# One value product for two heads on 64x64 tiles, with copies on ScalarE and TensorE steps of 640 instructions

## The chip, the cores and the metric

The kernel runs on one core of a Trainium2 chip. The metric is the device time in microseconds (us) of one execution. Before the change three runs took 4342.97, 4343.37 and 4332.03 us; the median is 4342.97 us. A further execution was profiled, and all views below are of it.

## The reference

A layer of two parts works on x, two images of 128 channels and 256x256 pixels, all in fp32.

```
x = x + conv_ref(ln_c(x), W_qkv, W_out, rel_height, rel_width)    # attention in windows
t = tokens of x
t = t + ffn_ref(ln_t(t), router_w, router_b, expert_w, expert_b)  # 8 experts, the best 2 weighted
```

In `conv_ref` the queries of an 8x8 window look at the keys and values of the 12x12 window around it, in 4 heads of 32 channels. A fixed mask leaves to each query only the keys whose row and column offsets have one parity. With it the window falls apart into four planes (row parity, column parity), in each of which 16 queries (4x4) look at 36 keys (6x6). The softmax of the scores weights the values, and `W_out` maps the result back:

```
attn = softmax(q @ k + rel_pos_emb + FIXED_MASK)
out  = attn @ v              # per window and head
return W_out @ out
```

In `ffn_ref` a router gives 8 probabilities per token, and the two best experts' outputs are added with normalised weights.

## The kernel before

The image is cut into strips of 8 rows, 64 strips over both images. Each strip has four parity planes, so the main loop makes 256 steps n. A plane of a strip has 4 rows and 128 columns: 512 queries, 32 windows of 16. Windows are taken in pairs whose key ranges are merged (6 rows, 10 columns, 60 keys in a slot of 64 partitions): 16 pairs, 8 in each half of the strip.

The order of work is written out by hand. The body of the loop advances generators (`next(score)`, `next(ahead)`, `next(attn)`, `next(norm)`, `next(outp)`) and interleaves them with the experts of an earlier row pair and with loads and stores; on every engine and in SP's DMA queue instructions run in that order. For TensorE a step n is:

- `scores` (L476, L493): the position terms of plane n, then the products of keys and queries. A tile takes 32 rows and 64 columns of the array; 4 heads and 2 halves make 8 tiles.
- `project` for plane n+1: values (`value_rows`, L349), relative logits (L408), keys (L422) and queries (L447), with the whole array.
- four expert products (L716) into the accumulator `acc`.
- `attend`: the softmax denominators (L514, the lhs is a block of ones with 32 columns), then the value products (L524, called PV below), one for each pair of windows, half and head: 64 products, each on 64 rows (keys) by 32 columns (the head's channels), with 32 queries streamed.
- the norm sums of a row (L582), three expert products (L716), the output projection `po` of plane n (L552), and the eighth expert product.

An fp32 product is two weight loads and two matmuls in the profile (PEld and PE), so the 64 value products are 128 of each.

PSUM tile `att` (4 banks, one buffer) holds the scores in its columns 0 to 255. ScalarE turns them to `pT` by one exp (L501). The value products and the denominators are then written to the columns 256 to 511 of the same tile (`av`). VectorE transposes the denominators (`sT`, L534), takes reciprocals (`rc`, L536), transposes them back (`rT`, L539) and multiplies: `o` = values times `rT` (L544). `o` is the moving operand of `po`. In the loop these three parts of `attend` stand at three places:

```
next(attn, None)      # L514 and the first half of L524
...                   # expert inputs xe on VectorE, DMA issues
next(attn, None)      # the second half of L524, sT, rc
next(attn, None)      # rT, o
```

ScalarE's order around this place is: the squares for the norm sums (L576), then what follows `next(attn)`, the one-column copy that paces the load of x (L114, its DMA is L115 on SP), later Ln and Exp for the norm (L235, L236).

From step 6 on each step begins with a directive to the loader (L825): it fills TensorE's instruction stream with empty slots until the next instruction lies at `BLOCK - FIRST_LIMIT` modulo `BLOCK`. With `BLOCK, FIRST_LIMIT = 256, 99` (L47) the first 99 instructions of a step are the last of a group of 256.

Of the kernel before, what the change touches and what calls it, by code (L numbers as in the profile page):

```python
# [13 lines left out]
ALU = mybir.AluOpType  # L14
# [4 lines left out]
HEADS, DH = 4, 32  # L19
# [24 lines left out]
KR, KC = 6, 10  # L44
NK = KR * KC
SLOT = 64
BLOCK, FIRST_LIMIT = 256, 99  # L47
NU = 9


# [1 line left out]
def kernel(  # L52
# [16 lines left out]
    nc = tc.nc  # L69
# [6 lines left out]
    HQ = NQ // 2  # L76
# [18 lines left out]
    def ctile(shape, name):  # L95
        return const.tile(shape, F32, tag=name, name=name)
# [48 lines left out]
    ones = ctile([P, 32], "ones")  # L145
# [28 lines left out]
    for rname, rsb in zip(("relh", "relw"), relsb):  # L174
# [4 lines left out]
        rT = ctile([P, n_rel], f"{rname}T")  # L179
# [6 lines left out]
    for h in range(HEADS):  # L186
        hp = slice(h * DH, (h + 1) * DH)
# [317 lines left out]
    def attend(n, state):  # L505


        att, pT, vv = state["att"], state["pT"], state["vv"]
        av = att[:, :, HQ:512]
        for half in range(2):  # L510
            rows = slice(half * SLOT, (half + 1) * SLOT)
            for h in range(HEADS):
                hp = slice(h * DH, (h + 1) * DH)
                nc.tensor.matmul(  # L514
                    av[hp, 2 + half], lhsT=ones[rows, :], rhs=pT[rows, h], start=True, stop=True
                )
        for t in range(HP):
            if t == HP // 2:
                yield
            for half in range(2):  # L520
                rows = slice(half * SLOT, (half + 1) * SLOT)
                for h in range(HEADS):
                    hp = slice(h * DH, (h + 1) * DH)
                    nc.tensor.matmul(  # L524
                        av[hp, half, 32 * t : 32 * t + 32],
                        lhsT=vv[rows, t, hp],
                        rhs=pT[rows, h, 32 * t : 32 * t + 32],
                        start=True,
                        stop=True,
                    )  # L530


        sT = work.tile([P, 2, HQ], F32, tag="sT", name=f"sT{n}", bufs=1)
        nc.vector.transpose(sT, av[:, 2:4])  # L534
        rc = small.tile([P, NQ // 32], F32, tag="rc", name=f"rc{n}")
        nc.vector.reciprocal(rc, sT.rearrange("p f (b k) -> p (f b) k", k=32)[:, :, 0])  # L536
        yield
        rT = work.tile([P, 2, HQ], F32, tag="rT", name=f"rT{n}", bufs=1)
        nc.vector.transpose(  # L539
            rT.rearrange("p f (b k) -> p (f b) k", k=32),  # L540
            rc.unsqueeze(2).broadcast_to([P, NQ // 32, 32]),
        )
        o = work.tile([P, 2, HQ], F32, tag="o", name=f"o{n}")
        nc.vector.tensor_tensor(o, av[:, 0:2], rT, ALU.mult)  # L544
        state["o"] = o
        yield

# [262 lines left out]
    with tc.manual_schedule(engines={ET.PE, ET.DVE, ET.Activation, ET.Pool, ET.SP}):  # L810
        for n in range(n_planes + 7):
            i, pl = divmod(n, 4)
            score, attn, outp, ahead, norm, rout = none, none, none, none, none, none
            if n < n_planes:
                score = scores(n, states[n])
                attn = attend(n, states[n])
                outp = out_project(n, states[n])
# [21 lines left out]
            if gated:  # L839
                f, c, made = gated  # L840
# [15 lines left out]
            f = (i - 1, pl) if 0 < i <= len(strips) else None  # L856
# [107 lines left out]
```

## Time and profile before

| | |
|---|---|
| median of 3 runs | 4342.97 us (4332.03 to 4343.37) |
| profiled execution, its own time | 4328.49 us |
| its span, first to last instruction | 4326.7 us |
| TensorE matmul busy | 4223.3 us, 98% |
| VectorE busy | 3791.0 us, 88% |
| ScalarE busy | 1320.7 us, 31% |
| L524, value products, matmuls | 32768, 346.7 us busy, mean 200 ns |
| L514, denominators, matmuls | 4096, 169.6 us busy, mean 388 ns |
| L544, o | 256, 177.0 us busy, mean 691 ns |
| mean granted TensorE clock | 0.991 |

Matmuls overlap one another, so a mean duration is longer than the distance from one start to the next; starts are what counts in a row of them. A timeline line gives start, length, engine, line, operation, tiles, form and count, and in brackets the idle time before it with what ended it. "issue" there is time in which the engine waited for nothing that the profile shows. Queue q8 carries instruction blocks to the engines; its packets are in the trace with start and length.

### The profile page before, as it was taken

To read this page: it belongs to the slowest core of one execution; us is meant where nothing else is said; L and a number is where in the kernel's file an instruction comes from. 1 tells how busy PE (TensorE), PEld (TensorE's weight loads), DVE (VectorE), ACT (ScalarE), POOL (GpSimd) and SP (SyncE) were. 2 spreads that over 40 slices of the span, in tenths; PEclk is the share of its full clock that TensorE was granted. 3 is DMA by queue.
4 is the path that set the end of the run, shared out by engine and by line. 5 is a ranking of instruction groups with operands and counts; after the bars stand their busy time and mean duration, and the time that the engine had idled before them with its cause. 6 is when DMAs were issued, how large, how long until landed. Compare 5 with 4: busy or idle time off the path is not lost. (4 is left out here: it accounts for less than half of the span.)

```text
span 4326.7 us, 224393 instructions
## 1 busy us (share of the span) xinstructions
PE 4223.3 (98%) x94273; PEld 2472.0 (57%) x94273; DVE 3791.0 (88%) x11850; ACT 1320.7 (31%) x3774; POOL 1087.6 (25%) x1126
## 2 busy tenths in 40 slices
PE   7899999999999999999999999999999999999987
PEld 5455555555555555555555555555555555555553
DVE  5788988988888889988888998898998889899877
ACT  3233332332323232333333233233332333333321
POOL 1222222222222222222222222222222222222211
PEclk8999999999999999999999999999999999999999
DMA  3777778787788778777778778778788787787866
GB/s 109 214 234 247 241 244 244 244 247 235 244 236 242 240 243 248 239 246 239 247 237 247 248 240 247 239 244 250 239 248 244 239 249 237 248 243 244 243 191 193
DMA packets 824578, 1022.17 MB, mean 236 GB/s; under 512 B 137634, under 2 KB 409634, under 8 KB 823594
## 3 DMA queue, kind: packets, MB, share of 16 engines
q1 hardware_dynamic: 822864, 1007.52, 75.9%
q8 instruction: 769, 12.60, 1.2%
q14 instruction: 215, 1.76, 0.1%
q10 hardware_dynamic: 730, 0.29, 0.0%
HBM read 863.78 MB, written 143.75 MB: 233 GB/s over the span
## 5 line engine op out<-in xcount | busy, mean ns | idle before, releaser
L716 PE MATMUL acc<-xe,ew 128*128 128x512 f32 x4096 | 1917.9, 601 | 18.6 <-DVE gb L690 14.3
L716 PEld LDWEIGHTS acc<-xe,ew 128*128 128x128 f32 x4096 | 758.4, 190 | 939.7 <-issue 873.1
L707 DVE TENSOR_TENSOR xe<-xs,gb 128x512 f32<-128x512 f32 x1536 | 950.8, 687 | 11.6 <-DMA gb<-gd 1.5
L711 POOL COPY last<-xe 128x1 f32<-128x1 f32 x256 | 47.6, 186 | 3115.3 <-DVE gb L690 3082.2
L707 POOL TENSOR_TENSOR xe<-xs,gb 128x512 f32<-128x512 f32 x512 | 652.3, 1275 | 1.5 <-PE att L524 1.2
L493 PE MATMUL att<-qs,kcol 32*64 32x32 f32 x32768 | 402.1, 227 | 15.8 <-issue 15.4
L493 PEld LDWEIGHTS att<-qs,kcol 32*64 32x64 f32 x32768 | 397.5, 132 | 19.6 <-issue 18.9
L275 POOL TENSOR_TENSOR xn<-xt,rb 128x512 f32<-128x512 f32 x249 | 374.3, 1503 | 94.6 <-DMA rb<-gd 94.0
L524 PEld LDWEIGHTS att<-pT,vwin 64*32 64x32 f32 x32768 | 349.4, 105 | 42.0 <-issue 4.5
L501 ACT ACTIVATE pT<-att 128x1024 f32<-128x1024 f32 x256 | 262.2, 1024 | 298.8 <-PE att L493 298.8
L524 PE MATMUL att<-pT,vwin 64*32 64x32 f32 x32768 | 346.7, 200 | 2.7 <-issue 1.5
L349 PE MATMUL pv<-wt,xn 128*128 128x128 f32 x2048 | 303.8, 292 | 0.6 <-issue 0.6
L412 DVE STREAM_TRANSPOSE uT<-pu 128x512 f32<-128x512 f32 x256 | 183.6, 717 | 134.9 <-PE pu L408 134.9
L576 ACT ACTIVATE sq<-xt 128x512 f32<-128x512 f32 x505 | 292.6, 630 | 0.0
L396 DVE STREAM_TRANSPOSE au<-auT 128x512 f32<-128x512 f32 x256 | 269.6, 1053 | 9.0
L552 PE MATMUL po<-o,wt 128*128 128x512 f32 x512 | 263.6, 596 | 10.2 <-DVE o L544 6.6
L433 ACT COPY kcol<-pk 128x560 f32<-128x560 f32 (+2 forms) x344 | 183.5, 533 | 275.0 <-PE pk L422 272.2
L408 PE MATMUL pu<-xn,wrel 128*128 128x512 f32 x512 | 267.2, 604 | 0.0
L447 PE MATMUL pq<-xn,wt 128*128 128x512 f32 x512 | 262.1, 592 | 1.7 <-issue 1.7
L422 PE MATMUL pk<-xn,wt 128*128 128x512 f32 (+2 forms) x528 | 261.5, 579 | 0.0
L349 PEld LDWEIGHTS pv<-wt,xn 128*128 128x128 f32 x2048 | 254.1, 195 | 11.5 <-issue 1.0
L476 PEld LDWEIGHTS att<-au,keys 32*64 32x64 f32 x8192 | 117.6, 132 | 228.2 <-PE po L552 183.8
(2437 smaller groups left out, 4856.6 us busy)
## 6 DMA issues: line engine op xcount, KB each, us to landing
gb<-gd SPq DMA_DIRECT2D x2048, 256.0 KB, 5.6
vwin<-vrows SPq DMA_DIRECT2D x512, 240.0 KB, 5.1
xt<-in_x_dram SPq DMA_DIRECT2D x256, 256.0 KB, 6.6
sb<-gd SPq DMA_DIRECT2D x256, 256.0 KB, 4.4
out_dram<-xt SPq DMA_DIRECT2D x256, 256.0 KB, 6.0
rb<-gd SPq DMA_DIRECT2D x249, 256.0 KB, 3.4
vrows<-vr SPq DMA_DIRECT2D x168, 256.0 KB, 3.8
vrows<-vr SPq DMA_DIRECT2D x160, 128.0 KB, 3.6
```

What stands on the lines that cost most here:

```text
L275: eng.tensor_tensor(xn[i % 2][:, :, :, k, 1 : PC + 1], ln1_src(i, k).rearrange("p (y j x) -> p y x j", y=2, x=2), rb.rearrange("p (y j x) ...
L349: nc.tensor.matmul(pv[:, j * P : (j + 1) * P], lhsT=xp[:, k, 1 : PC + 1], rhs=wv, start=True, stop=True,)
L396: nc.vector.transpose(au.rearrange("p m a s -> p a s m"), auT[n % 2])
L408: nc.tensor.matmul(pu, lhsT=wrel, rhs=inner, start=True, stop=True)
L447: nc.tensor.matmul(pq, lhsT=wq, rhs=inner, start=True, stop=True)
L493: nc.tensor.matmul(sc[rows, h, 32 * t : 32 * t + 32], lhsT=kk[hp, half * HP + t, :], rhs=qs[hp, m0 : m0 + 2].rearrange("p m a s -> p (m a ...
L501: nc.scalar.activation(pT, att[:, :, 0:HQ], AF.Exp)
L524: nc.tensor.matmul(av[hp, half, 32 * t : 32 * t + 32], lhsT=vv[rows, t, hp], rhs=pT[rows, h, 32 * t : 32 * t + 32], start=True, stop=True,)
L552: nc.tensor.matmul(po, lhsT=wo, rhs=state["o"].rearrange("p f z -> p (f z)"), start=True, stop=True)
L576: nc.scalar.activation(sq, src, AF.Square)
L707: eng.tensor_tensor(self.xe[e], self.xs, self.gb.pop(e), ALU.mult)
L716: nc.tensor.matmul(self.acc, lhsT=ew[:, e, :], rhs=self.xe.pop(e), start=(e == 0), stop=not self.xe)
```

## The change

The value products of two heads become one. The weights are the 64 channels of heads 2g and 2g+1, the moving operand is the 32 queries of both heads side by side (64 columns), and the output is 64 partitions by 64 columns: 32 products, on four tiles of 64 rows by 64 columns. Of each output half the elements are of use: for the even head's partitions the first run of 32 columns, for the odd head's the second. The outputs fill banks 0 and 1 of `att` from column 0, where the scores were. Two ScalarE copies (heads 1 and 3), from PSUM to PSUM, put the odd heads' runs over the mixed ones, so that `o` can read the first runs of all partitions. The denominators keep their place. `BLOCK` becomes 128 and `FIRST_LIMIT` 88.

```diff
-BLOCK, FIRST_LIMIT = 256, 99
+BLOCK, FIRST_LIMIT = 128, 88
...
-        av = att[:, :, HQ:512]
+        av = att[:, 2:4, HQ:512]
+        own = att[:, 0:2].rearrange("p f (t j z) -> p f t j z", j=2, z=32)
...
-                    av[hp, 2 + half], lhsT=ones[rows, :], rhs=pT[rows, h], start=True, stop=True
+                    av[hp, half], lhsT=ones[rows, :], rhs=pT[rows, h], start=True, stop=True
...
-                for h in range(HEADS):
-                    hp = slice(h * DH, (h + 1) * DH)
+                for g in range(2):
+                    gp = slice(2 * g * DH, 2 * (g + 1) * DH)
                     nc.tensor.matmul(
-                        av[hp, half, 32 * t : 32 * t + 32],
-                        lhsT=vv[rows, t, hp],
-                        rhs=pT[rows, h, 32 * t : 32 * t + 32],
+                        att[gp, half, 64 * t : 64 * t + 64],
+                        lhsT=vv[rows, t, gp],
+                        rhs=pT[rows, 2 * g : 2 * g + 2, 32 * t : 32 * t + 32],
...
-        nc.vector.transpose(sT, av[:, 2:4])
+        nc.vector.transpose(sT, av)
...
+        for h in (1, 3):
+            hp = slice(h * DH, (h + 1) * DH)
+            nc.scalar.copy(own[hp, :, :, 0], own[hp, :, :, 1])
...
-        nc.vector.tensor_tensor(o, av[:, 0:2], rT, ALU.mult)
+        nc.vector.tensor_tensor(
+            o.rearrange("p f (t z) -> p f t z", z=32),
+            own[:, :, :, 0],
+            rT.rearrange("p f (t z) -> p f t z", z=32),
+            ALU.mult,
+        )
```

## The prediction

> **What bounds the kernel now.** I read the page's engine shares first, then TensorE's timeline over one step, then the places where that timeline breaks, and last the packet records of the instruction queue.
>
> ```profile
> span 4326.7 us, 224393 instructions
> PE 4223.3 (98%) x94273; PEld 2472.0 (57%) x94273; DVE 3791.0 (88%) x11850; ACT 1320.7 (31%) x3774; POOL 1087.6 (25%) x1126
> ...
> q8 instruction: 769, 12.60, 1.2%
> ```
>
> TensorE is busy 98% of the span. The next view is its timeline over one step (start, length, line, count of matmuls).
>
> ```profile
> 1728.28 0.69 PE L476 MATMUL att<-au,keys 32*64 32x128 f32 x32
> 1728.77 1.53 PE L493 MATMUL att<-qs,kcol 32*64 32x32 f32 x128
> 1730.22 1.16 PE L349 MATMUL pv<-wt,xn 128*128 128x128 f32 x8
> 1731.22 1.02 PE L408 MATMUL pu<-xn,wrel 128*128 128x512 f32 x2
> 1732.08 1.02 PE L422 MATMUL pk<-xn,wt 128*128 128x512 f32 x2
> 1732.94 1.02 PE L447 MATMUL pq<-xn,wt 128*128 128x512 f32 x2
> 1733.80 3.59 PE L716 MATMUL acc<-xe,ew 128*128 128x512 f32 x8
> 1737.33 0.66 PE L514 MATMUL att<-pT,ones 64*32 64x256 f32 x16
> 1737.78 1.34 PE L524 MATMUL att<-pT,vwin 64*32 64x32 f32 x128
> 1739.05 0.43 PE L582 MATMUL plt<-xt,rw 128*32 128x128 f32 x8
> ...
> 1744.55 0.69 PE L476 MATMUL att<-au,keys 32*64 32x128 f32 x32
> ```
>
> There is no gap in it. The step takes 16.27 us, and 153 of the 248 steps with this sequence take that to 15 ns. TensorE is a hard floor, and what is added to or taken from its stream moves every step. The mean step is 16.50 us; the rest is stalls. Two kinds matter here, one in the step at 1065.73, one in the step at 1082.96:
>
> ```profile
> 1066.22 0.37 PE L493 MATMUL att<-qs,kcol 32*64 32x32 f32 x17
> 1067.36 1.34 PE L493 MATMUL att<-qs,kcol 32*64 32x32 f32 x111 [0.78 <-issue]
> ...
> 1088.48 1.45 PE L716 MATMUL acc<-xe,ew 128*128 128x512 f32 x3
> 1090.64 2.31 PE L716 MATMUL acc<-xe,ew 128*128 128x512 f32 x5 [0.71 <-issue]
> ```
>
> "issue" means that no semaphore held it. Count instructions (each product is two weight loads and two matmuls): L476 64, L493 256, L349 16, L408, L422 and L447 4 each, the first L716 group 16, L514 32, L524 256, and 84 after it, 736 in all. The first break comes after 32+17 matmuls and, by the weight loads' own timeline, 32+18 loads: 99 instructions, which is FIRST_LIMIT. The second comes after 348 and then 3 matmuls and 4 loads: 355 = 99+256. Breaks inside L524 sit near the third place, 611. So these are the ends of 256-instruction blocks, and q8's 769 fetches are three per step (768 slots). Its packets, set against the steps, give the law (steps 20 to 239; 35 stalls of the first kind):
> - TensorE resumes 1.31 to 1.57 us, median 1.44, after the **latest** fetch has landed. The next fetch starts only after that, 1.6 to 3.4 us later, median 2.8. So one block is held ahead, and a new one is asked for when the last is entered.
> - A step's first fetch lands at 4.67 us from its start (median; mean 4.70; 4.44 in steps of 16.27; tenths 3.97 and 5.42). It is usable at 6.1, for a block that is entered at 0.64. Fetching takes some 5.3 us. Instruction 355 is needed at 6.8, so it mostly arrives in time.
>
> **PV on 64x64 tiles.** L514 to L582 takes 1739.05-1737.33 = 1.72 us: 0.45 for L514, 1.27 for L524, whose 64 products start every 16.7 ns (1.07 us) with 0.2 for start and change of shape. Now there are 32 products on four tiles: 8 products, 16 passes a tile, each loading 64 columns and streaming 64. Streaming costs 0.43/512 us a column (L408), so 53 ns a pass; a 64-column load takes about 55 ns (mean loads 105, 132, 190 ns for 32, 64, 128 columns). Is the load hidden behind a stream of the same length? The nearest row is L349, 128 loaded and 128 streamed: its matmuls start every 112 ns, against 107 for the stream alone. It hides, with 5 ns left. So 16 x 57 ns = 0.91 us. L514 stays on 64x32, so a change of shape now stands between it and L524: from the last L582 matmul's start (32 columns) to the first of L716 (128) the records show 0.20 us, 0.09 beyond the stream of 0.11, and the first load is exposed (0.05). After: L514 0.50 + 0.09, first load 0.05, passes 0.91, tile offsets 0.02, change to L582 0.09 = 1.66 us. **Gain 0.06 us a step, 15 us in all.** Best bound, no change of shape and bare streaming: 0.45+0.87+0.11 = 1.43, gain 74 us. Worst, loads not hidden: 16 x 107 ns, 0.80 more, loss 190 us. I take the middle, by L349.
>
> [...]
>
> **The copies on ScalarE.** Two of 32 partitions x 512, by L449 (128x512 from PSUM, 0.59 us) and the pair at L576 (1.16 us for two) 1.1 us; bounds 0.4 (the L433 copy of 280 elements, 0.42) and 2.3 (twice).
>
> ```profile
> 1735.91 0.19 ACT L114 COPY xt<-onesm 128x1 f32<-128x1 f32 x1
> 1742.83 0.18 ACT L235 ACTIVATE r__103_33034<-plg 128x8 f32<-128x8 f32 x1 [6.73 <-DVE plg L234]
> ...
> 1741.04 0.69 DVE L544 TENSOR_TENSOR o<-att,rT 128x512 f32<-128x512 f32 x1
> ```
>
> ScalarE idles from 1736.1 to 1742.83. PV ends at 1739.05, the copies by 1740.3, before o starts at 1741.04; and o ends 1 us ahead of po (L552). Cost **0**; beyond 1.9 us the copies delay o, beyond 2.9 TensorE. Queued behind them are L114's pacing copy, now at 1740.3, and through it SP's load of x, which SP issues at 1742.31 anyway; then L235, at 1742.83. All are later. VectorE's reads keep their element counts: 0.
>
> **Steps of 640.** 736-128 = 608 instructions, padded to a multiple of 128: 640 (32 empty slots, as before 768-736; they show no time between L716 and L476). 640 is two and a half blocks, so block ends fall by turns at 88, 344 and 600 of one step and at 216 and 472 of the next.
> - *88 to 344.* Slot 88 is entered at 0.60 us. Slot 344 is L447's first load, right after L422; its matmul starts at 1732.94-1728.28 = 4.66. The block lands at 4.70-0.05 (mean), is usable 1.44 later, and the load is exposed (0.11): 6.2. Stall 1.5 us by all steps, 1.2 by the undisturbed ones; I take 1.25, since the step before lacks this stall. Bounds: 0.8, if every fetch were like the quickest tenth (3.97), and 1.9, like the upper quartile (5.05). With 125 such steps: **+156 us** (100 to 238).
> - *600 to 216.* 600 is entered while the second L582/L716 stretch runs, at 11.1 to 11.7 us (L722 releases L716 at 11.1). 216 is needed in L493, 1.35 us into the next step, at 16.21+1.35 = 17.56, 5.9 to 6.5 us later. The third fetch of a step before lands 4.2 us (mean) after 611 is entered at 10.46 and is usable 1.44 later, 5.6 in all. Its 220 delays, laid against this need, give a mean wait of 0.15 to 0.34 us; I take 0.25, **+31 us** (0, if the late ones vanish, to 100, if 600 is entered a product later, at 12.6).
> - *Gone:* stalls at 99 (23 us summed, about 4 stay, since 472 is entered earlier), at 355 (6) and at 611 (7): **-32 us**.
>
> [...]
>
> Sum, against the profiled run's 4328.5 us (span 4326.7): -15+156+31-32 = +140, 4468. The three runs' median, 4343, is 14 above the profiled one, two of three at 4343; I add half: **4475 us**.
>
> **The rivals.**
> 1. *Blocks arrive in time* (the breaks are something else, or the fetch runs further ahead): only the PV gain and the vanished stalls are left, 4328.5-15-32 = 4282, with the half offset of 7 to the runs' median **4290**, faster. It decides where entry-to-usable falls below 4.1 us (0.60 to 4.66); hardly one step in a hundred before is so quick. 11%.
> 2. *Weight loads not hidden* on 64x64, on top of the forecast: PV loses 190 instead of gaining 15, 4475+205 = **4680**. 4%.
> 3. *The copies late*: they decide from 2.9 us after PV's end. At four times L449's time (4.4 us) po would be 1.5 late in every step, 4475+256x1.5-31 = **4830**. 1%.
> 4. *The padding is not what it says*: with 768 slots and ends at 88, 344, 600 every step would have the long stall, 4475-31+156 = **4600**. 2%.
>
> Forecast 80%. Range 4380 to 4640: below, the stall's low bound (4475-56) with most of PV's best bound (-59); above, its high bound (+82) with 100 instead of 31 for slot 216, and rival 4. It leaves out rivals 1 to 3 and the outer edge of the forecast, some 2 in 10. A time within 0.3% (13 us, what this kernel's runs can tell from no change) needs the stall and PV gain to cancel: 2%. Faster is rival 1, 11%; slower the rest, 87%.
>
> **What would show it.** In every second step TensorE idles 1 to 1.5 us ahead of L447, released by "issue", and steps go 17.5, 16.3, 17.5; q8 has about 645 fetches; L524 has 16384 matmuls, starting every 14 ns. ScalarE's copies end before o, and VectorE's share falls. I am wrong if L447 shows no idle: then the fetch law fails. If L524 grows to some 2 us, the loads are exposed.

## The result, and the profile after

The changed kernel takes 4911.84 us (median of 4 runs, 4894.65 to 4933.64). The kernel before, run beside it, takes 4340.97 us (4 runs). The ratio is 1.132 (95% interval 1.130 to 1.134). The forecast was 4475 us with a range up to 4640: the sign was right, and 437 us were missing.

All views of after are of its profiled execution: 4933.64 us, 605 above the profiled one of before. The page first: span, engine shares, instruction queue.

```profile
span 4931.9 us, 192022 instructions
PE 4456.2 (90%) x77889; PEld 2529.6 (51%) x77889; DVE 3804.2 (77%) x11850; ACT 1614.8 (33%) x4286; POOL 1088.9 (22%) x1126
q8 instruction: 641, 10.50, 0.9%
```

TensorE has 16384 matmuls fewer, yet its busy time has grown by 233 us, and it idles on top of that. The instruction queue makes 641 fetches, two and a half a step, as forecast. The groups of that page (busy us, mean ns, then the idle time ahead of them and what ended it) name the lines. From here on line numbers are those of after: denominators L515, value products L525, sT L535, copies L540, o L548, experts L725.

```profile
L493 PE MATMUL att<-qs,kcol 32*64 32x32 f32 x32768 | 437.1, 231 | 260.1 <-issue 260.1
L422 PE MATMUL pk<-xn,wt 128*128 128x512 f32 (+2 forms) x528 | 324.1, 666 | 135.7 <-issue 135.7
L525 PE MATMUL att<-pT,vwin 64*64 64x64 f32 x16384 | 297.3, 221 | 0.0
```

The forecast stall is there, in L422 and not ahead of L447 (135.7 us), and no idle time lies ahead of the value products. But the scores L493, before 15.8 us, now wait 260.1 us for "issue". TensorE's timeline over an odd step (from 2212.91) and the even one behind it shows both places.

```profile
2212.91 0.69 PE L476 MATMUL att<-au,keys 32*64 32x128 f32 x32
...
2216.72 0.59 PE L422 MATMUL pk<-xn,wt 128*128 128x512 f32 x1
2219.01 0.59 PE L422 MATMUL pk<-xn,wt 128*128 128x512 f32 x1 [1.70 <-issue]
2219.43 1.02 PE L447 MATMUL pq<-xn,wt 128*128 128x512 f32 x2
2220.29 3.59 PE L725 MATMUL acc<-xe,ew 128*128 128x512 f32 x8
2223.82 0.66 PE L515 MATMUL att<-pT,ones 64*32 64x256 f32 x16
2224.41 1.16 PE L525 MATMUL att<-pT,vwin 64*64 64x64 f32 x64
2225.50 0.43 PE L591 MATMUL plt<-xt,rw 128*32 128x128 f32 x8
...
2226.51 2.84 PE L725 MATMUL acc<-xe,ew 128*128 128x512 f32 x6
...
2231.00 0.69 PE L476 MATMUL att<-au,keys 32*64 32x128 f32 x32
2231.49 0.98 PE L493 MATMUL att<-qs,kcol 32*64 32x32 f32 x75
2235.10 1.08 PE L493 MATMUL att<-qs,kcol 32*64 32x32 f32 x53 [2.63 <-issue]
2236.11 2.08 PE L349 MATMUL pv<-wt,xn 128*128 128x128 f32 x8
2237.98 1.91 PE L408 MATMUL pu<-xn,wrel 128*128 128x512 f32 x2
```

In the odd step the break lies between the two matmuls of L422, one matmul ahead of the computed slot 344. The trace of after has a semaphore wait of TensorE's sequencer at L476 in each step (256 of them, none before), which the count left out; with it, and the load that runs ahead, L422's second matmul is the first thing behind slot 344. In the even step the break lies after 32+75 matmuls, so after 214 instructions, the semaphore wait and one more load: slot 216. Behind that wait everything is slow: L349's eight matmuls take 2.08 us (1.16 before), L408's two 1.91 (1.02). The table of stretches gives the reason (length, PE busy with count, granted clock, DMA share, GB/s):

```profile
2231.00:2235.10 4.10, 1.47 (x108) 0.97 0.89 284
2235.10:2241.40 6.30, 6.30 (x66) 0.50 0.16 53
2241.40:2253.10 11.70, 11.70 (x133) 0.99 0.83 231
```

After the wait the granted clock is 0.50 for 6.3 us. In the clock records of steps 10 to 245 this half rate lasts 3.41 or 6.83 us each time, 433 us in all (3.4 before). Each time it begins within a wait of TensorE or at most 2 us behind one. It follows 103 of the 198 waits of over 0.9 us (median 2.1 us), and not the other 95 (median 1.4 us); of the 81 waits over 2 us it follows 73. No sharp bound separates them.

Over steps 10 to 245, odd steps take 17.60 us on average, even ones 20.25; an undisturbed step, one without such waits, takes 16.23 (16.27 before). So +1.37 x 118 = 162 us in odd steps and +4.02 x 118 = 474 in even ones; less 0.04 x 236 = 9 for the value products and 37 for the stalls that before had in these steps, that is some 590 of the 605 us.

The ScalarE copies, in the list of waits (engine, tile, line waited for: us in all, times, longest):

```profile
ACT att L540 <- DVE sT L535: 1067.4, 256, 5.1
DVE o L548 <- ACT att L540: 44.3, 256, 0.2
```

They start only after sT, and o waits 0.17 us for them in each step. TensorE's floor doesn't show it.

### The profile page after: what moved, and what is told of

Same layout as the page of the kernel before. It is cut to its first block, busy times and chain, and to the rows that moved or that the text cites. A ratio compares the mean times of both kernels' runs of the same rounds, so it can differ in the third digit from the quotient of the medians.

```text
span 4931.9 us, 192022 instructions
## 1 busy us (share of the span) xinstructions
PE 4456.2 (90%) x77889; PEld 2529.6 (51%) x77889; DVE 3804.2 (77%) x11850; ACT 1614.8 (33%) x4286; POOL 1088.9 (22%) x1126
## 5 line engine op out<-in xcount | busy, mean ns | idle before, releaser
L725 PE MATMUL acc<-xe,ew 128*128 128x512 f32 x4096 | 1913.9, 600 | 16.5 <-DVE gb L699 14.9
L725 PEld LDWEIGHTS acc<-xe,ew 128*128 128x128 f32 x4096 | 758.2, 190 | 935.7 <-issue 867.8
L493 PE MATMUL att<-qs,kcol 32*64 32x32 f32 x32768 | 437.1, 231 | 260.1 <-issue 260.1
L540 ACT COPY att<-att 32x512 f32<-32x512 f32 x512 | 283.7, 554 | 1075.5 <-DVE sT L535 1067.4
L493 PEld LDWEIGHTS att<-qs,kcol 32*64 32x64 f32 x32768 | 422.9, 137 | 272.4 <-issue 272.3
L422 PE MATMUL pk<-xn,wt 128*128 128x512 f32 (+2 forms) x528 | 324.1, 666 | 135.7 <-issue 135.7
L349 PE MATMUL pv<-wt,xn 128*128 128x128 f32 x2048 | 378.3, 341 | 0.8 <-issue 0.8
L408 PE MATMUL pu<-xn,wrel 128*128 128x512 f32 x512 | 350.4, 774 | 4.4 <-issue 4.4
L349 PEld LDWEIGHTS pv<-wt,xn 128*128 128x128 f32 x2048 | 318.1, 237 | 13.0 <-issue 1.2
L525 PEld LDWEIGHTS att<-pT,vwin 64*64 64x64 f32 x16384 | 262.2, 134 | 105.4 <-DMA sb<-gd 43.6
L535 DVE STREAM_TRANSPOSE sT<-att 128x512 f32<-128x512 f32 x256 | 183.0, 715 | 164.9 <-PE att L525 164.2
L525 PE MATMUL att<-pT,vwin 64*64 64x64 f32 x16384 | 297.3, 221 | 0.0
```

The lines of the kernel that those rows point to most:

```text
L349: nc.tensor.matmul(pv[:, j * P : (j + 1) * P], lhsT=xp[:, k, 1 : PC + 1], rhs=wv, start=True, stop=True,)
L408: nc.tensor.matmul(pu, lhsT=wrel, rhs=inner, start=True, stop=True)
L422: nc.tensor.matmul(pk[:, : m * PC], lhsT=wk, rhs=xp[:, part[0] : part[0] + m, 1 : PC + 1], start=True, stop=True,)
L493: nc.tensor.matmul(sc[rows, h, 32 * t : 32 * t + 32], lhsT=kk[hp, half * HP + t, :], rhs=qs[hp, m0 : m0 + 2].rearrange("p m a s -> p (m a ...
L525: nc.tensor.matmul(att[gp, half, 64 * t : 64 * t + 64], lhsT=vv[rows, t, gp], rhs=pT[rows, 2 * g : 2 * g + 2, 32 * t : 32 * t + 32], start ...
L540: nc.scalar.copy(own[hp, :, :, 0], own[hp, :, :, 1])
```

## The experiments

The theory behind the first runs: the products and copies are neutral; everything lost is instruction blocks that come late, at slot 344 in odd steps and at slot 216 in even ones, and the half clock follows the latter. The rival: the new products or copies cost time themselves. Later runs ask why the block for slot 216 is so late: because slot 600 is entered late, or because other transfers keep the DMA engines busy. Times are medians; ratios are to the kernel before in the same series (4330.6 to 4340.2 us).

**Blocks as before, with empty slots.**

```diff
-BLOCK, FIRST_LIMIT = 128, 88
+BLOCK, FIRST_LIMIT = 256, 99
...
+        if 6 <= n < n_planes:      # behind the value products
+            nc.tensor.addr_align(BLOCK, offset=(653 - FIRST_LIMIT) % BLOCK)
```

> The new value products and the ScalarE copies are all in; BLOCK and FIRST_LIMIT are 256 and 99 again, and a second alignment puts 128 empty slots behind the last value product, so that block ends lie at slots 99, 355 and 611 of every step, the last in the empty slots, entered at some 10.6 us. Theory (all of the loss is late instruction blocks and the clock that drops after them): floor step 16.23 us as in the changed kernel, 0.04 under before, stalls as before; 4331 us, 4315 to 4345. Rival (the 64x64 products or the copies cost time of their own): 4400 or more.

Measured 7027.69 us, ratio 1.622 (1.619 to 1.624). A miss: the 128 empty slots behind the value products are not free. They run 71 ns apart, hold TensorE for some 9.1 us a step, and the granted clock falls with it (0.813 over the span). Every step takes 27.3 us, so nothing is told about the theory. The idle time stands ahead of the norm sums (L592 in this run and in the third):

```profile
L592 PE MATMUL plt<-xt,rw 128*32 128x128 f32 x4040 | 335.0, 416 | 2269.4 <-issue 2269.4
```

**The old products with the first limit at 88.** In the kernel before:

```diff
-BLOCK, FIRST_LIMIT = 256, 99
+BLOCK, FIRST_LIMIT = 256, 88
```

> The kernel before with one number changed, FIRST_LIMIT 88 instead of 99 (BLOCK 256): block ends at 88, 344 and 600 of every step. No 64x64 product, no copy. Theory: every step has the stall ahead of the second L422 or L447 matmul that every second step of the changed kernel has (1.36 us a step there): 4341 + 250 x 1.36 = 4680 us, 4600 to 4750. Rival (the products or the copies are the cause): 4341.

Measured 4565.66 us, ratio 1.053 (1.050 to 1.057), below the forecast range.

```profile
L447 PE MATMUL pq<-xn,wt 128*128 128x512 f32 x512 | 287.4, 643 | 181.7 <-ACT kcol L443 101.4 <-ACT kcol L433 47.2 <-issue 32.4
```

The row puts most of this wait down to ScalarE's copies, which end at about that time. But it ends 1.41 us (median; nine in ten between 1.26 and 1.58) after a fetch has landed, as the waits of after do (1.40 us), and the kernel before, with the same copies, has 1.7 us there. So the wait at slot 344 comes with the limit alone, without 64x64 tiles, new copies or steps of 640; a mean step takes 17.42 us, 1.0 more than before (1.37 in odd steps of after). The place is confirmed, the size over-estimated.

**Slot 600 entered earlier.** After, with 28 empty slots behind the value products:

```diff
+        if 6 <= n < n_planes:
+            nc.tensor.addr_align(BLOCK, offset=(553 - FIRST_LIMIT) % BLOCK)
```

> The changed kernel with 28 of its empty slots moved from the step's end to behind the last value product. Slot 600 then lies in L591 and is entered at some 11.4 us instead of with the third product of L725; 88, 344, 216 and 472 stay. Theory (the block after 600 is asked for too late, because TensorE's sequencer enters it hardly ahead of the work): the steps with slot 216 fall from 20.25 to 16.5 us, and with them most of the half-rate clock goes: 4912 - 125 x 3.7 = 4450 us, 4420 to 4520. Rival (the fetch is slow for the DMA traffic at that place, or the stall at 216 is the stall of 344 handed on): 4850 or more.

Measured 4782.08 us, ratio 1.104 (1.102 to 1.106). The time was missed; the wait that the run was to cure is gone. The groups of the scores and of the norm sums, and the mean granted clock:

```profile
L493 PE MATMUL att<-qs,kcol 32*64 32x32 f32 x32768 | 394.5, 226 | 4.8 <-issue 4.6
L592 PE MATMUL plt<-xt,rw 128*32 128x128 f32 x4040 | 216.4, 278 | 409.0 <-DVE rc L538 397.8 <-issue 4.6 <-DVE rT L544 3.8
core 0: 4778.1 us, clock 0.993
```

The wait in L493 has gone from 260.1 us to 4.8, and the half clock with it (0.946 to 0.993). What was not expected is the price of the 28 empty slots there: TensorE idles 409 us ahead of the norm sums, 1.64 us in each of 250 steps, nearly what the cured stall cost; the undisturbed step is 17.91 us. The row names VectorE's `rc`, but the trace has the 28 slots in just this gap, 71 ns apart as in the first run, 2.0 us in all, of which 0.35 pass while value products still run. With a longer step the run does not show the earlier entry alone: from the weight load at slot 600 (13.8 us, 14.95 in after, both with the stall at 344) 6.3 us remain to slot 216, not 4.0, and the fetch starts 2.3 us after that load, not 3.9.

**The same with limit 104,** which moves slot 344 to 360, into the first expert group: `BLOCK, FIRST_LIMIT = 128, 104`, and the directive above.

> As the run before with FIRST_LIMIT 104: block ends at 104, 360, 616 (in L591's last products, entered at some 11.6 us) and at 232, 488. Slot 360 lies in the first L725 group and is needed at 7.7 us instead of 4.2. Theory: both stalls go, all steps near 16.23 us: 4320 us, 4305 to 4345. Rival (steps of two and a half blocks cost time wherever the ends lie): 4400 or more.

Measured 4770.59 us, ratio 1.101 (1.098 to 1.103), a miss in time. The empty slots cost the same (undisturbed step 17.89 us). The wait in L422 is gone (0.0 us of idle time ahead of it, 135.7 in after): odd steps take 17.91. Even ones take 18.64; 65 of 118 have a wait at slot 232, where 216 was, of 0.7 us (median).

**The empty slots hidden.** After, limit 104, 29 empty slots ahead of the denominators, where eight expert matmuls of 3.6 us are queued ahead:

```diff
-BLOCK, FIRST_LIMIT = 128, 88
+BLOCK, FIRST_LIMIT = 128, 104
...
+        if 6 <= n < n_planes - 1 and strips[(n + 1) // 4][1] > 0:   # ahead of L515
+            nc.tensor.addr_align(BLOCK, offset=(394 - FIRST_LIMIT) % BLOCK)
```

> BLOCK 128, FIRST_LIMIT 104 as in the run before, but 29 of the 31 empty slots stand ahead of the denominators (L515), behind the first group of L725, instead of behind the value products. The runs before showed that an empty slot costs TensorE's sequencer about 60 ns (28 of them 1.66 us, 128 of them 9.1 us) where the matmuls queued ahead do not cover it. Theory: the 3.5 us of L725 cover them, the floor is 16.23 us again, slot 360 is in time, and slot 616 is entered at some 11.5 us, before the step's DMA burst: 4325 us, 4310 to 4380. Rival (the empty slots are not covered there either): 18.0 us a step, 4770.

Measured 4542.8 us, ratio 1.047 (1.045 to 1.050), a miss. Here the slots cost nothing: odd steps take 16.25 us. Of 118 even steps 35 have no wait in the scores; the other 83 wait 2.2 us (median), and 45 of them take 20 us or more. The mean is 18.66. A slow one, in TensorE's timeline:

```profile
2288.31 1.05 PE L493 MATMUL att<-qs,kcol 32*64 32x32 f32 x83
2291.85 0.70 PE L493 MATMUL att<-qs,kcol 32*64 32x32 f32 x45 [2.49 <-issue]
```

32+83 matmuls are 230 instructions: slot 232. Slot 616 is reached at 11.4 us of the odd step (its weight load), and yet the block that is asked for there is late in two cases of three. Where it is in time its fetch starts at 14.7 us of the odd step (median, 16.0 at the latest), where it is late at 17.5 (15.6 at the earliest). So an earlier entry alone doesn't settle it.

**Half and a quarter of the gates' traffic.** After, with the transfers of the gates `gb` cut to half (the gates of the second half of the tokens are left out, the first half's are used twice) and then to a quarter. The edit of the quarter:

```diff
-            nc.sync.dma_start(self.gb[e], to_all(self.gd, e))
+            half = self.gd[e * NT : e * NT + 1].rearrange("r k -> (r k)")
+            nc.sync.dma_start(self.gb[e][:, 0:P], half.partition_broadcast(P))
```

> The changed kernel, with each of the eight gate transfers a step (gb from gd) halved, 128 KB instead of 256, and the first half used for both; this leaves out the second half's gates. A quarter of the DMA traffic goes, TensorE's stream stays. Theory A (the block after slot 600 is late because its fetch waits behind the DMA burst that starts at some 12 us of a step and fills the 16 engines until 18): its fetch starts 1.5 to 3 us sooner, steps with slot 216 fall from 20.25 to 18 us or less, and the stall at 344 shrinks a little too: 4600 or less. Theory B (it is late only because slot 600 is entered late): steps with slot 216 stay within 0.5 us, 4850 or more.

> The changed kernel with each gate transfer cut to a quarter (64 KB, the first 128 of 512 columns used for all); this leaves out the gates of three quarters of the tokens. With halves the burst still filled the DMA engines from 12 to 15 us, and steps with slot 216 fell from 20.25 to 18.82 us. Theory (the fetch waits behind the burst): with quarters hardly any burst is left, steps with slot 216 fall to 17.2 us or less, steps with slot 344 to some 17.0: 4440 us, 4370 to 4500. Rival (late entry alone, a fetch that takes its time anyway): steps with slot 216 stay above 18.3, 4600 or more.

Measured 4687.45 us, ratio 1.082 (1.080 to 1.084), and 4606.1 us, ratio 1.063 (1.061 to 1.066). Even steps fall from 20.25 us to 18.82 and 18.32. The first result lies between its two theories; the second is a miss, on the side of its rival (above 18.3 us and 4600). Less traffic helps, but neither run comes near the floor. The median time from the start of instruction 598, just ahead of slot 600, to the start of the next fetch goes from 3.97 us to 3.45 and 3.31.

**No alignment.** After without the directive at the head of a step: steps of 608 instructions and two semaphore waits, whose block ends wander.

> The changed kernel without the alignment directive: steps of 610 slots, so that block ends drift by 98 slots a step through all places. Theory: no empty slots and no fixed bad place; some steps have one or two late blocks, others none, 1.0 to 2.0 us a step in the mean: 4600 to 4850. Rival (the alignment itself, its empty slots at the step's end, is the cost): 4340 or less.

Measured 4630.15 us, ratio 1.068 (1.066 to 1.071), in the forecast range. Left to themselves the block ends cost less than the alignment to 640: half of the steps are near the floor (median 16.7 us), the others much longer.

**Steps filled up to 736.** After with the blocks of before, and 32 one-column products repeated behind the value products, so that the step has as many instructions as before (no empty slot is exposed):

```diff
-BLOCK, FIRST_LIMIT = 128, 88
+BLOCK, FIRST_LIMIT = 256, 99
...
+        for t in range(4):
+            for half in range(2):
...
+                for h in range(HEADS):
...
+                    nc.tensor.matmul(
+                        att[hp, half, c0 : c0 + 1],
```

> The changed kernel's value products and copies, with BLOCK 256 and FIRST_LIMIT 99 as before the change, and 32 products of one column each (repeats of values already written, 64x32 tiles) behind them, so that the step has 736 instructions again and block ends lie where they lay before. The repeats cost 32 x 16.7 ns and a change of tile shape, some 0.65 us a step. Theory (the 64x64 products and the copies cost nothing by themselves, 0.04 us less than before): floor 16.9 us, 4333 + 256 x 0.63 = 4495, 4470 to 4530. Rival (they cost time of their own): 4580 or more.

Measured 4471.87 us, ratio 1.032 (1.030 to 1.034): as expected. The filler is seen in one step of the timeline, and the rest has the stalls of before, no more (steps 10 to 245 lie 26 us in all above the undisturbed step, before 37):

```profile
2224.93 1.16 PE L525 MATMUL att<-pT,vwin 64*64 64x64 f32 x64
2226.02 0.70 PE L539 MATMUL att<-pT,vwin 64*32 64x1 f32 x64
```

The undisturbed step is 16.86 us, 0.63 more than after's. 256 x 0.63 = 161; 4471.9-161 = 4311, 0.5% below the kernel before. So the new products and copies, without the late blocks, cost nothing, and the rival falls.

**Queries later.** Limit 104 and hidden slots as above, and the query products L447 (0.86 us) moved behind the norm sums, so that the last block of a step is entered sooner; and the same move alone in the kernel before:

```diff
             next(ahead, None)
-            next(ahead, None)
...
             next(norm, None)
...
             next(ahead, None)
+            next(ahead, None)
```

> As the run with 104 and the empty slots ahead of the denominators, with one more move: the query product (L447, 0.86 us, 4 instructions) and its ScalarE copy stand behind L593, the norm sums, and no longer ahead of the first expert products. Slot 616 is then entered with that product, at some 10.9 us of the step and not 11.7, before the DMA burst. In the run before it, steps with slot 232 either lost nothing or 2 us and more, by whether the fetch started by 15.8 us or after the burst. Theory: most of them now fetch in time, floor 16.23 us, mean 16.3 to 16.5: 4290 us, 4275 to 4340, faster than the kernel before. Rival (the half of the steps with slot 232 that lost was set by something else than the time of entry): 4500 or more.

> The kernel before, with the same move of the query product and nothing else: no 64x64 product, no copy, BLOCK 256, FIRST_LIMIT 99. Slot 611 is entered 0.86 us sooner. Theory: the stalls at 99 (23 us summed) mostly go, the floor stays at 16.27: 4310 us, 4295 to 4330. Rival (the move delays the next step's scores or VectorE): 4345 or more. Against the run above it tells what the 64x64 products are worth where the blocks arrive.

Both are misses: 4559.02 us, ratio 1.052 (1.050 to 1.055), and 4393.29 us, ratio 1.015 (1.013 to 1.017). In the first, even steps still spread (36 of 118 without a wait, mean 18.72 us) though the block is entered at 10.9 us, 0.5 earlier than in the run with the hidden slots; its fetch starts no sooner (17.4 us, median, against 17.1). In the second, the stall at slot 99 is gone (2.4 us ahead of L493), but with L447's 0.86 us gone from ahead of it slot 611 is needed sooner:

```profile
L524 PE MATMUL att<-pT,vwin 64*32 64x32 f32 x32768 | 366.0, 200 | 72.8 <-issue 71.3
```

Before, 2.7 us stood there. Here the move of a product took the stall from one block's end to another.

**Branching over the empty slots.** After with the blocks of before; the 128 spare slots lie ahead of the denominators, and the loader puts a branch over them:

```diff
-BLOCK, FIRST_LIMIT = 128, 88
+BLOCK, FIRST_LIMIT = 256, 99
...
+        if 6 <= n < n_planes - 1 and strips[(n + 1) // 4][1] > 0:
+            nc.tensor.addr_align(BLOCK, offset=(365 + 128 - FIRST_LIMIT) % BLOCK, max_nops=0)
```

> New value products and copies, blocks of 256 with the step's block ends at 99, 355 and 611 as in the kernel before; the empty slots lie in the middle of the step, ahead of the denominators, and the loader's branch goes over them instead of TensorE's sequencer working through them. Late-blocks theory: the step is at its floor of 16.23 us but for the stalls that the kernel before has too, so 4320 us (4305 to 4345), 0.2% below the kernel before. Rival, that a jump within a step costs a fetch of its own or the half clock (2 us or more a step): 4850 us or more. Rival, that the value products on 64x64 tiles and ScalarE's copies cost time by themselves: above 4400 us with no stall in the scores.

Measured 4375.05 us, ratio 1.008 (1.006 to 1.010). Undisturbed steps take 16.23 us, so the branch costs nothing there, and 537 of the 572 us that the change lost are back. The forecast that it would beat the kernel before fails: in the expert group ahead of the branch and the value products behind it some waits are longer than before (16 and 28 us in all, 6 and 6 before), and where the images meet, where no branch is placed, 128 empty slots stand exposed in four steps, 35 us in all, as much as the whole difference to the kernel before. One of them:

```profile
2226.05 1.16 PE L476 MATMUL att<-au,keys 32*64 32x128 f32 x32 [8.70 <-issue]
```

**Early entry and quartered traffic together.**

> The changed kernel with the block ends moved by 104 in place of 88, the 29 empty slots ahead of the denominators, and the gates' transfers cut to a quarter (the gates of three quarters of the tokens are left out). Theory that late entry and DMA backlog both make the wait: the block for slot 232 is asked for by 10.3 us and fetched at once, every step takes 16.23 to 16.4 us, no half clock, 4280 us (4265 to 4320). Rival, that the fetch has a delay of its own that follows neither: half of the even steps still wait 2 us or more, 4500 us or more. Rival, that the gates' share of the backlog is small beside the values' and the inputs' transfers: in between, even steps at 17 us, 4360 us.

Measured 4340.98 us, ratio 1.001 (1.000 to 1.003): it misses the theory's 4320 us and lies nearest to the last rival (4360, even steps at 17 us); the rival of a delay that follows neither falls. Odd steps stand at 16.24 us, even ones at 16.93, and what is left is mostly a short wait in the scores (70 of 118 even steps, median 0.8 us):

```profile
2268.93 0.70 PE L493 MATMUL att<-qs,kcol 32*64 32x32 f32 x45 [0.54 <-issue]
```

The four kernels make a square of even steps (us):

| | all gates | a quarter |
|---|---|---|
| slot 600 as in the change | 20.25 | 18.32 |
| slot 616, reached some 2.2 us earlier | 18.66 | 16.93 |

Early entry is worth 1.6 and 1.4 us, less traffic 1.9 and 1.7. They nearly add up, and 0.7 us above the floor are explained by neither. The lower row has the limit 104 and so no stall in L422 either; its odd steps are over 1 us shorter with all gates (16.25 against 17.60), so it is not the entry alone that differs between the rows.

## Why the prediction was wrong

**What held.** TensorE as the floor: the undisturbed step fell by 0.04 us (0.06 forecast), with the denominators at 592 ns (590) and the value products at 1091 (1070); their passes start every 58 ns (57). The loads on 64x64 tiles are hidden, as L349's row (a start every 112 ns) said: a pass of load and stream one after the other would take 107 by the prediction's estimate. 641 fetches; the block ends at 88, 344, 600 and 216, 472. Odd steps lose 1.37 us against 1.25. The forecast named an idle L447 as its sign; the idle time is one matmul earlier, by the semaphore wait that it did not count. Copies at no cost on the path, though by another order: they wait for sT, so they start at 2226.49, 0.99 us after the value products, and o waits 0.17 us, but still ends 0.84 us ahead of po (2228.35 against 2229.19). Slower, and by none of the rivals: the blocks come late, the loads are hidden, `o` is in time, and 641 fetches are not steps of 768 slots.

**The step that failed** is "600 to 216", +31 us in the sum; it cost 474. Three things were wrong in it.

1. The place of slot 600. The forecast let it be entered "at 11.1 to 11.7 us". Counted through: 524 instructions up to the end of the value products, 64 of norm sums, 12 of the six expert matmuls make 600, so it stands at the end of that expert group (with the semaphore wait at L476 it is the weight load of the sixth matmul). In the timeline above the group starts at 2226.51, 11.9 us into the step without its stall, and the weight load of its last matmul runs at 13.6 (median over the odd steps: 14.95, less the stall of 1.37). Slot 216 is needed at 17.56, so 4.0 us remain, not 5.9 to 6.5. By the forecast's own 5.6 us from entry to use this alone is a wait of 1.6 us, some 200 us over 125 steps. The upper bound of the term, "a product later, at 12.6", lay short of the place too.

2. The delay of the fetch. The 5.6 us came from the third fetch of before, asked for at 10.46 us, whose start followed the entry by 2.6 us (median). The fetch for slot 216 is asked for while the DMA engines are full (share 0.94 to 1.0 in each us from 12 to 18 of an odd step, by the packets) and starts 3.97 us after instruction 598 has started. The wait is therefore 2.1 us on average (260.1 us in 125 waits). The runs with less traffic and with the earlier entry show that both matter. How the fetch gets its turn among the other transfers, and why the earlier entry of the hidden-slots run left 83 waits in 118 even steps, stays open: there slot 616 is reached at 11.4 us and the fetch starts 5.7 us (median) later, so its start does not simply follow the entry.

3. The half clock. A wait of that size was priced by its own length. After it, some 3.4 to 6.8 us often run at 0.50, and the step loses the difference: 4.02-2.08 = 1.94 us per even step, 229 us in all. Half of the 433 us at half rate, 217, agrees with that. The sum had no term for it: the kernel before has three waits over 0.9 us in steps 10 to 245, and one stretch of half rate.

The range failed with the term: its upper end held 100 us for slot 216, for a place that was itself wrong.

## What to carry to other kernels

When a change alters the number of instructions, count each block's end through to the instruction it falls on and read that instruction's time in the timeline, for every one of the alternating ends. Here the end entered late in the step (13.6 us in, where the DMA engines' share is 0.94 to 1.0) cost most: 474 us, against 162 for the one entered at its start. Price a long wait of TensorE with the half clock that may follow it: here it followed 73 of 81 waits over 2 us, and 30 of 117 from 0.9 to 2 us. In these runs empty slots were hidden only behind queued matmuls of 0.43 us (odd steps of 16.25 us with 29 of them there); 28 behind the value products cost 1.64 us a step. A branch over 128 of them cost less (4375 us) than work in their place (4472).

## What was not expected of the hardware

- An empty slot in TensorE's stream takes its sequencer 71 ns, in the traces of before, after and the runs with 128, 28 and 29 slots moved (28 slots 2.0 us, 128 slots 9.1 us); 29 to 31 of them show no time where expert matmuls of 0.43 us each are queued ahead (31 a step in before, 30 in after, with no gap ahead of L476; 29 in the run with the hidden slots, whose odd steps take 16.25 us against after's undisturbed 16.23). Undisturbed steps with a branch over 128 take 16.23 us too.
- In steps 10 to 245 of after the half rate (granted clock 0.50) comes in pieces of 3.41 us, one or two of them, after 103 of 198 waits over 0.9 us.
